# A four-layer graph network on one core: list building in layer 0 at one and a half steps per group instead of two

## The chip, the cores and the metric

The kernel runs on one core of a Trainium2 chip. The metric is the device time of one launch in microseconds (us): 1701.81 us, the median of three runs (1696.1 to 1703.36).

## The reference, cut to what matters

A graph of 3327 nodes has an adjacency matrix `adj` of ones and zeros and node features `x` of width 512. Four layers follow each other; each computes `x = layernorm(x + layer(x, adj))`.

```python
# layer 0: attention with 8 heads of 64
Wh = einsum('nd,hdo->hno', x, W);  f1 = Wh . a1;  f2 = Wh . a2
e = leaky_relu(f1[:, :, None] + f2[:, None, :], 0.2), where adj > 0, else -9e15
out = elu(softmax(e) @ Wh)
# layer 1: mean over all neighbours, two dense products, one combining product, relu
# layer 2: mean over the first 64 neighbours, a dense product on each side, leaky relu
# layer 3: attention with 4 heads of 128 on a quaternion weight
```

Edges are many in the first rows and few in the last: node i is joined to node j with a chance proportional to 1/sqrt((1+i)(1+j)).

## The kernel before, in words

**Tiling.** The nodes are cut into 26 blocks of 128. For blocks 1 to 25 the kernel doesn't use the dense matrix: it builds an edge list for each block (`lists`, a class `EdgeList`), with one entry per edge, in chunks of 128 edges. Block 0, the densest, is treated apart, with whole rows of the matrix (`dense`).

**List building** is the Python generator `structure` (its instructions are on lines 861 to 982). For each block it fetches the adjacency rows (L874, two halves on the SP queue, one pair of buffers), takes their sign on ScalarE (L881, `masks`), multiplies by a position code (L896), finds the columns with repeated maxima on VectorE (L909, L919, L921), counts places with small matmuls (L931, L932, L943), spreads them to edge places with matmuls `pv` (L960) and comparisons (L968 to L975), and writes the list (L978 to L981). It stops (`yield`) five times per block, so a list is five steps. The function `more(n)` takes n such steps; `ready` is the place, in the order of blocks, of the last list that is done.

**Layer 0** has two stages. In the first, 26 blocks are loaded, transposed and multiplied by the weights, and a table `t0_d` of rows is written; each block brings three steps of list building. In the second, the table's rows are gathered, edge by edge. A loop goes over groups of up to four chunks (`feed`, `groups`): there are 63 such groups, for 201 chunks in all, in 25 blocks. A group is a generator too (`Gat.group`): gathers on POOL (L1005), distances on ScalarE (L1267), choice of edges on VectorE (L1275, L1277), scores on TensorE (L1287) and transposed choice (L1297), reduction and maximum on VectorE (L1303 to L1306), exponentials on ScalarE (L1307, L1308), a copy of the choice to SBUF (L1310), the multiply of gathered rows by the weights on VectorE (L1315, one per group), and the sums on TensorE (L1334). When a block's groups are done its end follows (`layer0_end`): normalization on VectorE and ScalarE (L1485 to L1498, L857), and two dense products into `po` (L797) whose results go to `t1_d` and `z1_d` through the SP queue.

**The loop around the change** takes one group, moves every living generator one stage on (`work.step()`), and then calls `more`. At its start 17 of 26 places are ready, so nine lists, 45 steps, are left. A group whose list isn't ready yet would build on demand:

```python
            while ready < order.index(item[0]):
                more()
            work.add(g0.group(item, pools, accs, layer0))
        work.step()
        more(2)
```

When the last list is done (`ready == NB - 1`), the buffers of the building are closed, and their space goes to weights of layer 2, which are loaded (L1688) and transposed on TensorE (L1697) and copied by ScalarE (L1698) as one more generator, `transposed_weights`. Block 0's dense work (L1437, L1444) starts with the last seven blocks, when 18 of 25 blocks have been passed on.

**What sets the order.** The program text isn't the order on the engines. In layer 0 a scheduler at build time places each engine's instructions, by their dependences and the order in which they were written; every engine then runs its own list in order. From layer 1 on the order is that of the text. In the second stage of layer 0 the pool `l0p1` has one buffer for each of its names, and `banks.shared` gives the building's matmuls `pv` the buffer `po` of the dense products, and its transposes and sums (`lp`) the buffer `tr` of the transposes.

Of the kernel before, what the change touches and what calls it, by code (L numbers as in the profile page):

```python
# [631 lines left out]
def sparse_path(ctx, tc, flag_i, x, adj, l0_w, l0_a1, l0_a2, l1_w_self, l1_b_self, l1_w_nb, l1_b_nb,  # L632
# [26 lines left out]
    def pool_in(lay, name, bufs=1, **kw):  # L659
        return lay.enter_context(tc.tile_pool(name=name, bufs=bufs, reuse_waits="tile", **kw))  # L660
# [880 lines left out]
    with ExitStack() as pro:  # L1541
# [83 lines left out]
        def more(n=1):  # L1625
            nonlocal ready, whole
            for k in range(n):
                b = next(made, None)
                whole = b is not None or ready == NB - 1
                ready = ready if b is None else b  # L1630
# [50 lines left out]
    def transposed_weights():  # L1681

        n = len(raws) - 2
        jobs = [(src, o, k) for src, o in ((l2_w_nb, wn2), (l2_w_line, wl2)) for k in range(DC)]

        def fetch(i):
            src, _, k = jobs[i]
            nc.sync.dma_start(raws[i % n], src[k * P:(k + 1) * P, :])  # L1688

        for i in range(n):  # L1690
            fetch(i)
        yield
        for i, (_, o, k) in enumerate(jobs):
            yield
            pt = ps.tile([P, DC, P], F32, name="pt", tag="tr")
            for c in range(DC):
                nc.tensor.transpose(pt[:, c, :], raws[i % n][:, c * P:(c + 1) * P], ident)  # L1697
            nc.scalar.copy(o[:, :, k * P:(k + 1) * P], pt)  # L1698
            if i + n < len(jobs):
                fetch(i + n)  # L1700

    w2lay, dlay = ExitStack(), ExitStack()
    def feed():

        left = list(range(NB))
        blocks = [b for b in order if b]
        for n, b in enumerate(blocks):
            if n == len(blocks) - DENSE - 2:
                assert wn2 is not None
                dp = pool_in(dlay, "l0d")  # L1710
                work.add(g0.open_dense(fin, ps, pools[2], dp.tile([P, H0 * P], F32, name="up"),
                                       *[raws[-1 - k] for k in range(2)],
                                       *[dp.tile([P, H0 * g0.M], F32, name=f"gd{k}") for k in range(3)]))
            for item in groups(pools[0], (b,), True):
                yield item
                for _ in range(2):
                    if left and n >= len(blocks) - DENSE:
                        yield left.pop(0)
        yield from left

    for k, item in enumerate(feed()):
        if isinstance(item, int):
            work.add(g0.dense(item, fin, ps, pools[2], layer0))
        else:
            while ready < order.index(item[0]):
                more()
            work.add(g0.group(item, pools, accs, layer0))
        work.step()
        more(2)
        if ready == NB - 1 and wn2 is None:  # L1730
            listlay.close()
            aside = pool_in(ctx, "s_more")
            wp = pool_in(w2lay, "l2w")
            wn2 = wp.tile([P, DC, D], F32, name="wn2")
            wl2 = wp.tile([P, DC, D], F32, name="wl2")
            places = aside.tile([P, MORE], F32, name="raw", tag="aside")
            raws = [places[:, k * D:(k + 1) * D] for k in range(2)]
            raws += [places[:, (k + 1) * H0 * P:(k + 2) * H0 * P] for k in range(2)]
            work.add(transposed_weights())
# [356 lines left out]
@with_exitstack  # L2096
def kernel(ctx: ExitStack, tc: tile.TileContext, *args):


    nc = tc.nc  # L2100
    pool = ctx.enter_context(tc.tile_pool(name="flagp", bufs=1))
    flag_i = pool.tile([1, 1], I32, name="flag_i")
    sparse_path(tc, flag_i, *args)
    again = nc.values_load(flag_i[0:1, 0:1], min_val=0, max_val=1 << 20)
    with tc.If(again > 0):
        general_path(tc, *args)
# [30 lines left out]
```

## Time and profile before

| what | value |
|---|---|
| median of three runs | 1701.81 us |
| the profiled execution, its time | 1795.35 us |
| its span, first to last instruction | 1793.6 us |
| TensorE busy | 1513.9 us, 84% |
| VectorE busy | 1220.8 us, 68% |
| ScalarE busy | 876.6 us, 49% |
| POOL busy | 762.9 us, 43% |
| mean granted TensorE clock | 0.932 |
| groups of gathers of layer 0 (L1315) | 250 to 713 us |
| last write of an edge list (L980) | 398 us |

How to read it: times in the profile count from the first instruction of the span. A line such as L1315 is a line of the kernel's text; PE is TensorE's matmul, PEld its weight load, DVE is VectorE, ACT is ScalarE, POOL is GpSimd, SP is the engine that only issues transfers. A row of a group gives engine, operation, output and inputs with their shapes, how often it ran, its busy time and mean duration, and the engine's idle time just before it with what ended most of it. Row sums of VectorE and ScalarE are larger than the engine's busy time, because one instruction's end overlaps the next one's start. The busy time of TensorE is modelled, and a busy TensorE isn't one at its peak.

### The profile page before, as it was taken

Reading aid. Unit: us, or ns where it says so; the run is one execution under the profiler, and the core shown is the slowest. Engines: PE = TensorE matmul, PEld = TensorE weight load, DVE = VectorE, ACT = ScalarE, POOL = GpSimd, SP = SyncE. Lnnn points to the kernel's source line nnn. Section 1 sums busy time; section 2 is a strip of 40 time slices with the busy share of each in tenths; the row PEclk is TensorE's granted clock in tenths of the full one; section 3 lists DMA queues with packets and bytes.
Section 4 is the critical chain, followed back from the end, with each engine's and each line's share of the span. In section 5 each row is a group of like instructions: output and inputs, shape, how many; then the busy total and the mean of one; then the engine's idle time right before and its main releaser. Section 6 shows DMA issues by size and latency. Waiting matters only on the chain. (4 is left out here: it accounts for less than half of the span.)

```text
span 1793.6 us, 24341 instructions
## 1 busy us (share of the span) xinstructions
PE 1513.9 (84%) x7263; PEld 1007.8 (56%) x7298; DVE 1220.8 (68%) x3289; ACT 876.6 (49%) x2921; POOL 762.9 (43%) x904
## 2 busy tenths in 40 slices
PE   5979937789999999889999998856999984788784
PEld 4756526556666667345555554423666662666663
DVE  8989859996668788135665675537655533687896
ACT  5879645656566677311221221102444442476785
POOL 2000144555555510264545552366667106666540
PEclk9989968999999999989999998988999995999897
DMA  8787766766564531398889894387888207677761
GB/s 265 248 266 241 210 192 232 207 189 205 173 200 153 178 113 61 144 401 289 291 283 357 274 319 182 132 285 246 260 263 278 92 37 199 196 209 211 214 182 44
DMA packets 130402, 381.99 MB, mean 213 GB/s; under 512 B 22037, under 2 KB 36477, under 8 KB 130259
## 3 DMA queue, kind: packets, MB, share of 16 engines
q0 software_dynamic: 67696, 252.97, 44.8%
q1 hardware_dynamic: 62563, 127.35, 21.1%
q8 instruction: 60, 0.98, 0.2%
q14 instruction: 83, 0.68, 0.1%
HBM read 331.89 MB, written 48.37 MB: 212 GB/s over the span
## 5 line engine op out<-in xcount | busy, mean ns | idle before, releaser
L1005 POOL DMA_INDIRECT gl<-t_d,idx x270 | 270.5, 1002 | 272.2 <-DMA e_d<-es 81.0
L1005 POOL DMA_INDIRECT gt<-t_d,idx x201 | 200.5, 998 | 377.4 <-DVE g0fall L845 199.7
L1334 PE MATMUL acc<-gt,sel 128*128 128x264 f32 (+3 forms) x804 | 213.0, 412 | 3.1 <-issue 1.8
L797 PE MATMUL po<-wn,xt 128*128 128x512 f32 x416 | 193.6, 607 | 11.0 <-ACT xt L785 5.7
L1005 POOL DMA_INDIRECT gm<-t_d,idx x136 | 137.7, 1012 | 136.9 <-PE acc L1810 81.8
L1334 PEld LDWEIGHTS acc<-gt,sel 128*128 128x128 f32 (+3 forms) x804 | 154.4, 201 | 43.9 <-issue 17.0
L1334 PE MATMUL acc<-gl,sel 128*128 128x260 f32 (+3 forms) x544 | 147.6, 416 | 29.5 <-issue 21.9
L1334 PEld LDWEIGHTS acc<-gl,sel 128*128 128x128 f32 (+3 forms) x544 | 105.9, 204 | 52.4 <-issue 26.1
L797 PEld LDWEIGHTS po<-wn,xt 128*128 128x128 f32 x416 | 78.7, 195 | 94.6 <-issue 76.2
L1042 PE MATMUL po<-gt,xt 128*128 128x268 f32 x416 | 115.7, 423 | 14.8 <-ACT xt L789 11.2
L1315 DVE TENSOR_TENSOR gt<-gt,pg 128x1536 f32<-128x1536 f32 (+3 forms) x63 | 116.4, 1848 | 15.4 <-ACT sel L1310 14.7
L785 ACT COPY xt<-pt 128x512 f32<-128x512 f32 x81 | 46.7, 588 | 140.3 <-PE pt L782 108.4
L1810 PE MATMUL acc<-gm,selr 128*128 128x512 f32 (+4 forms) x324 | 107.2, 454 | 5.4 <-DMA gm<-t_d,idx 3.6
L909 DVE MAX8 cand<-val 128x8 f32<-128x464 uint16 (+32 forms) x184 | 107.7, 619 | 0.0
L1042 PE MATMUL po<-w,xt 128*128 128x262 f32 x416 | 99.5, 393 | 6.3 <-ACT xt L789 5.1
L1042 PEld LDWEIGHTS po<-gt,xt 128*128 128x128 f32 x416 | 78.4, 202 | 34.1 <-ACT xt L789 14.5
L1267 ACT ACTIVATE far<-place,nmids 128x128 int16<-128x128 int16 (+3 forms) x167 | 88.0, 544 | 18.2 <-DVE ds L1277 10.1
L797 PE MATMUL po<-wx,xt 128*128 128x512 f32 x208 | 93.7, 595 | 2.1 <-DVE t L1669 1.8
L797 PE MATMUL po<-wl,xt 128*128 128x512 f32 x208 | 93.5, 594 | 2.0 <-DVE tb L1877 1.3
L1042 PEld LDWEIGHTS po<-w,xt 128*128 128x128 f32 x416 | 78.8, 192 | 25.2 <-ACT xt L789 7.5
L782 PE MATMUL pt<-s_ident,xres 128*128 128x128 f32 x500 | 79.1, 287 | 13.3 <-DVE xres L852 10.0
L881 ACT ACTIVATE m<-ab 128x1664 bf16<-128x1664 int32 x50 | 80.2, 1605 | 16.9 <-DMA ab<-in_adj_dram 13.2
(372 smaller groups left out, 3238.8 us busy)
## 6 DMA issues: line engine op xcount, KB each, us to landing
ab<-in_adj_dram SPq DMA_DIRECT2D x25, 832.0 KB
ab<-in_adj_dram SPq DMA_DIRECT2D x25, 831.5 KB
t_d<-t SPq DMA_DIRECT2D x25, 512.0 KB
gm<-t_d POOLq DMA_DIRECT2D x25, 512.0 KB
t_d<-t SPq DMA_DIRECT2D x25, 384.0 KB
t_d<-tg SPq DMA_DIRECT2D x25, 264.0 KB
gd<-t_d SPq DMA_DIRECT2D x25, 264.0 KB
t_d<-tg SPq DMA_DIRECT2D x25, 260.0 KB
```

The lines of the kernel that those rows point to most:

```text
L782: nc.tensor.transpose(pt[:, c, :], src[:, c * P:(c + 1) * P], ident)
L785: nc.scalar.copy(xt, pt)
L797: nc.tensor.matmul(po, xt[:, c, :], w[:, c], start=c == 0, stop=c == DC - 1)
L881: nc.scalar.activation(m, ab[s], AF.Sign, accum_out=half[:, s, b:b + 1])
L909: nc.vector.max(out=cand[:, s, :], in_=val[:, cuts[s]:cuts[s + 1]])
L1005: nc.gpsimd.indirect_dma_start(out=t[:m, c, :], out_offset=None, in_=table[:, :], in_offset=bass.IndirectOffsetOnAxis(ap=l.idx[:m, c0 + c: ...
L1042: nc.tensor.matmul(pw[s], xt[:, c, :], self.w[:, c, s, :], start=c == 0, stop=c == DC - 1)
L1267: nc.scalar.activation(o, place[:, (c0 + q0) * P:(c0 + q1) * P], AF.Abs, bias=l.nmid[:, k:k + 1], scale=2.0)
L1315: nc.vector.tensor_mul(Gc[:, :, :OUT], Gc[:, :, :OUT], w[:, :g].rearrange("p c (h o) -> p (c h) o", o=1).to_broadcast([P, g * H, OUT]))
L1334: nc.tensor.matmul(accs[b][s], S[:m, c, :], G[:m, c, s * hh * M:(s + 1) * hh * M], start=at + c == 0, stop=last)
L1810: nc.tensor.matmul(accs[b], chosen, parts[:, k * D:(k + 1) * D], start=at + c + k == 0, stop=k == top and at + c == n - 1)
```

## The change

The loop takes one step of list building after every even group and two after every odd one. The 45 steps then end with the 30th group instead of the 23rd; the eight transposes of layer 2's weights, which follow the last list, begin that many groups later. The dense work of block 0 keeps its place.

```diff
             work.add(g0.group(item, pools, accs, layer0))
         work.step()
-        more(2)
+        more(1 + k % 2)
         if ready == NB - 1 and wn2 is None:
             listlay.close()
             aside = pool_in(ctx, "s_more")
```

## The prediction

> **What bounds the kernel now.** I first read the busy shares of the page in forty slices of 44.8 us, to find the stage that the edit touches. Groups of gathers run from about 250 us to 713 us; list building among them ends at about 398 us, where the last write of an edge list (L980) stands. That is slices 5 to 8 (counted from 0).
>
> ```profile
> PE   5979937789999999889999998856999984788784
> DVE  8989859996668788135665675537655533687896
> PEclk9989968999999999989999998988999995999897
> ```
>
> Slices 6 to 8 have VectorE at 9 and TensorE at 7 or 8; from slice 9 TensorE is at 9 and VectorE falls to 6. So I cut the trace at 405, 455 and 545 us, and asked for the busy times (columns: length, PE, PEld, DVE, ACT, POOL, clock, DMA share, GB/s).
>
> ```profile
> 250.00:405.00 155.00, 122.75 (x656) 89.72 (x657) 140.40 (x471) 93.70 (x276) 77.53 (x82) 0.88 0.68 206
> 405.00:455.00 50.00, 50.00 (x240) 34.55 (x240) 32.35 (x80) 33.52 (x105) 26.38 (x30) 1.00 0.68 205
> 455.00:545.00 90.00, 89.18 (x380) 58.54 (x379) 60.38 (x150) 54.59 (x169) 51.17 (x64) 1.00 0.59 182
> ```
>
> While lists are built VectorE is busy 140.4 of 155 us (90.6%) and TensorE 122.75; afterwards TensorE has no idle time at all. Then the waits of TensorE in 250 to 405 us (total us, times, longest):
>
> ```profile
> PE pg L1287 <- DVE gt L1315: 23.6, 9, 8.8
> PE p L931 <- DVE dg L929: 4.3, 2, 3.3
> PE pv L960 <- ACT u L953: 2.5, 1, 2.5
> PE pv L960 <- ACT dl L945: 2.4, 2, 2.1
> PE po L797 <- DVE t L1669: 1.5, 1, 1.5
> PE pv L960 <- ACT vc L963: 1.4, 1, 1.4
> PE po L797 <- ACT vc L963: 1.2, 2, 0.9
> ```
>
> TensorE waits chiefly for VectorE's multiply of gathered rows (L1315), the one big VectorE instruction of each group. In 405 to 455 us the same view has no wait of TensorE. Last, VectorE's costliest groups in 250 to 405 us, and the transposes of layer 2's weights, which follow the building:
>
> ```profile
> L1315 DVE TENSOR_TENSOR gt<-gt,pg 128x2048 f32<-128x2048 f32 (+1 forms) x22 | 44.3, 2012 | 0.3 <-ACT sel L1310 0.3
> L909 DVE MAX8 cand<-val 128x8 f32<-128x1018 uint16 (+5 forms) x43 | 30.4, 736 | 0.0
> L896 DVE TENSOR_TENSOR val<-m,code 128x1664 uint16<-128x1664 bf16 x14 | 14.1, 1011 | 0.0
> L946 DVE TENSOR_TENSOR dl<-p,dl 128x26 bf16<-128x26 f32 x9 | 1.6, 182 | 4.5 <-ACT dl L945 3.7 <-issue 0.7
> ...
> L1697 PE MATMUL pt<-s_ident,raw x32: 272/273/421, 397.2 to 448.5; 128*128 128x128 f32 x32
> ```
>
> Two stages, then: 23 groups in 160 us (the first L1315 starts at 250, the 23rd at 410), 7.0 us each, set by VectorE; and from there 22 groups in 135 us (the 45th at 545), 6.1 us each, set by TensorE.
>
> **What the Trainium skill says.** "Perfetto Trace Analysis", Optimization Strategy: a kernel may have regimes with different most-contended engines, and interleaving them may help. The trace has just these two regimes. "TensorE: Matmul & The Clock Gate", Part 1: an idle window of about 3.4 us puts the clock back to half. The trace agrees in direction: with waits up to 8.8 us the granted clock was 0.88 in the first stage, and 1.00 afterwards. The same page's table has VectorE as a strict first-in first-out queue; the L946 row agrees (4.5 us idle in nine places with other groups' work behind). "Perfetto Trace Analysis", Matmuls: independent matmul groups should rotate through PSUM banks. Here the building's pv and the dense products' po share one buffer, and the waits of po for vc (1.2 us) and for t (1.5 us) are that price so far.
>
> **The change part by part.** Nothing is computed anew: the same 45 steps (nine lists of five) stay, one or two per group in turn instead of two. They are used up in 30 groups instead of 23. Sizes and waits on `ready` stay the same: in program order no group comes to the loop that builds on demand, in either kernel (list 17 is due before block 17, which begins with the 46th group). What moves is read from the order of instructions on each engine, which is the same again from about the 39th group on.
>
> VectorE. Ahead of the 23rd L1315 stand 946 building instructions in the kernel before, 899 in the changed one: 47 fewer, among them two L896, six L909, 39 small ones. By the rows: 2 x 1.01 + 6 x 0.74 + 39 x 0.19 (the small rows run 0.15 to 0.25) = 13.9 us. Row sums overlap: all VectorE rows of 250 to 405 us add up to 176 us where the engine is busy 140.4, so times 0.80, 11 us. At 90.6% use that brings the 23rd group from 410 to 398 us: **-12 us**. But by the 25th L1315 only 23 small ones are missing (23 x 0.19 x 0.8 = 3.5 us): the order lets two L896 and six L909 catch up between groups 23 and 25. Between these VectorE has then 11 - 3.5 = 7.5 us of building on top of 2.5 us for each group (the group's rows add up to 70.5 us for 23, times 0.80) and one layer end of 3.2 us (15.8 us for four, times 0.80): 16 us, where the kernel before took 10 us (410 to 420). So the 25th group comes at 414 instead of 420: **-6 us**.
>
> TensorE. From there it sets the pace in both. By the 25th group the kernel before had done 20 of the 32 weight transposes, the changed one none. All 32 took 5.3 us busy (1.06 up to 405 us, 4.23 after), so 20 cost 3.3 us, and the last 12 of the pv matmuls 0.7 us (7.0 us for 120 in their row): **+4 us**, uncovered, because TensorE has no idle time left to hide them. Before, some of the transposes went into its idle time before 405 us.
>
> Waits. TensorE's waits on the building (p, pv, and po behind vc) were 4.3 + 2.5 + 2.4 + 1.4 + 1.2 = 11.8 us for eight lists, 1.5 us a list, then free behind VectorE. About 0.7 of a list's small tail falls into TensorE's stage: **+1 us**; bounds 0 and, if each is lengthened threefold by a fuller ScalarE queue, 3.
>
> Clock. The first groups meet TensorE less idle, so its clock may rise sooner; VectorE sets the pace there, so I take 0, with 2 us of gain as the bound.
>
> DMA. Of SP, the last two lists' adjacency loads (L874) now stand after stores of t1 and z1, and the weight loads (L1688) among later stores. The store ahead of such a load waits for a result whose ScalarE part stands ahead of the mask that frees the load's own buffer, so the queue adds nothing I can find: 0. Without that cover a late load holds mask L881 at the head of ScalarE, and everything behind it; one load lasts about 10 us, for at most two lists. POOL's gathers keep their order; two memsets (L872) and square roots move among them by a few places: 0.
>
> Sum: -6 + 4 + 1 = **-1 us** of the profiled execution. Two favourable roundings stand beside it: VectorE may run the long catch-up above 95% busy (-1), and some transposes may slip into TensorE's waits on the last lists (-1). I take -3. That execution took 1795.35 us, with a span of 1793.6; the median of the runs is 1701.81, 5.2% less. A shift of 3 us carries over as 3 us: **1699 us**. Dense work of row 0 and everything after the 39th group has the same order, and starts 3 us sooner.
>
> **The rivals.**
>
> *The relief is kept.* VectorE's work is evened out and TensorE follows. 250 to 455 us have 140.4 + 32.35 = 172.75 us of VectorE; at 90.6% that is 190.7 us instead of 205, -14; transposes +5, so -9. If chains of small building steps also hide better between groups (VectorE at 95%: 182 us), -18. Middle: 1688 us. For it: 32 us of TensorE idle in the first stage. Against: the order gives back most of the building by the 25th group.
>
> *The first stage keeps its pace, and the second pays.* If the first 23 groups are held by latencies from engine to engine, not by VectorE's work, taking half a step from each saves nothing. Then all 32 transposes and the waits and pv matmuls of 2.2 lists (at the 20th L1315, 70 building instructions of some 31 a list are missing) land where TensorE is full: 5.3 + 2.2 x 1.5 + 1 = +10, so 1712 us. It decides from the point where the first 25 groups gain less than the 4 to 5 us that TensorE is handed. For it: of the fourteen ten-us windows from 250 to 390 us, four show VectorE at 87% or less. Against: 90.6% over all.
>
> *Nothing is seen.* List building has slack everywhere: 1702 us. It falls in with my forecast within the measurement.
>
> **How the numbers follow.** My forecast, with the case of no effect, has 0.5 (own range 1693 to 1709), the kept relief 0.24, the payment 0.26. One half per cent (8.5 us: 1693.3 to 1710.3) is about what a measurement of this kernel can tell from no change. The relief case lies mostly below, the payment case mostly above, a little of each inside, and a little of the forecast outside: faster 0.23, same 0.52, slower 0.25. The range reaches to the middle of each rival and somewhat beyond on the slow side, for a late load: 1685 to 1717.
>
> **What would show it.** Right: the 23rd L1315 starts some 12 us earlier than 410, the 25th some 6, the 35th 2 or 3; VectorE is above 85% busy until about 430 us, transposes (L1697) run from about 445 to 490 us, TensorE has new waits there for vc, u or dl; from the 45th group all intervals are as before. Wrong on the good side: TensorE's total wait in 250 to 455 us drops by over 10 us. Wrong on the bad side: the 25th group is not earlier, or masks (L881) wait for the adjacency. If dense work (L1444) changes its intervals, I have missed a dependence altogether.

## The result, and the profile after

| | before | changed |
|---|---|---|
| median of 13 runs | 1701.69 us | 1692.47 us |
| lowest to highest | 1695.88 to 1704.8 us | 1687.15 to 1695.45 us |
| ratio to before, 95% interval | 1 | 0.9947, 0.9934 to 0.9959 |
| the profiled execution, its time | 1795.35 us | 1689.52 us |

The changed kernel is 9.2 us (0.53%) faster. The two first profiles can't be subtracted: that of before comes from an execution of 1795 us, that of the changed kernel from one of 1690 us. In the later experiments the runs of both kernels took some 1790 us, and there the ratio came out the same (0.995). So the stages are compared on profiles from those, one of each kernel.

First the page of the changed kernel's first profile, busy shares in forty slices (of 42.2 us, since its span is 1687.8 us):

```profile
PE   5979987989999989889999999787999996888884
DVE  7998979988668789316556677547666644789996
PEclk9989989999999999879999999899999997999998
```

From slice 6 on VectorE has 9, 9, 8, 8, 6, and TensorE 7, 9, 8, 9, 9; before it was 9, 9, 9, 6, 6 and 7, 7, 8, 9, 9. The step from one engine to the other is softer. (The slices of the two pages differ in length, so this is no more than an impression.)

Now the pair: a further profile of the kernel before (span 1783.2 us) and one of the changed kernel (1788.8 us). The pair understates the gain. The execution of before was 5.5 us shorter than the median of the runs taken with it (1790.46), that of the changed kernel 3.1 us longer than its own (1787.47). Both profiles are cut at the start of the first, 23rd, 30th and 45th L1315, rounded to whole microseconds (columns: length, PE, PEld, DVE, ACT, POOL, clock, DMA share, GB/s). The kernel before:

```profile
249.00:408.00 159.00, 126.99 (x678) 92.19 (x679) 142.09 (x480) 98.29 (x293) 80.74 (x84) 0.89 0.68 209
408.00:452.00 44.00, 44.00 (x217) 31.25 (x216) 29.44 (x68) 27.41 (x82) 23.57 (x27) 1.00 0.66 198
452.00:542.00 90.00, 89.59 (x382) 58.86 (x381) 61.03 (x150) 55.16 (x173) 52.07 (x64) 1.00 0.60 184
```

The changed kernel:

```profile
248.00:393.00 145.00, 119.93 (x640) 86.86 (x641) 130.03 (x412) 89.25 (x256) 81.04 (x84) 0.92 0.70 219
393.00:441.00 48.00, 44.52 (x222) 30.56 (x222) 39.68 (x130) 31.22 (x108) 24.92 (x28) 0.96 0.66 195
441.00:537.00 96.00, 94.05 (x415) 62.14 (x413) 64.02 (x156) 60.19 (x184) 51.22 (x62) 1.00 0.61 185
```

The stretch to the 23rd group is 14 us shorter (13.2 before rounding), with 12 us less of VectorE's work in them. The next seven carry 10 us more of it and take 4 us longer, and the fifteen after that take 6 us longer: the weight transposes stand there now. In the stretch as a whole TensorE is idle for 30.5 us instead of 32.4 (length less busy, the three rows added), and its busy time is 258.5 us instead of 260.6, with a higher granted clock in the first row (0.92 for 0.89) and a lower one in the second (0.96 for 1.00).

The waits of TensorE, before, in the first row's window (total us, times, longest):

```profile
PE pg L1287 <- DVE gt L1315: 14.9, 8, 4.2
PE pg L1287 <- DVE nmids L940: 6.7, 1, 6.7
PE p L931 <- DVE dg L929: 3.3, 1, 3.3
```

And the two largest of the changed kernel in its first row, 248 to 393 us:

```profile
PE pg L1287 <- DVE gt L1315: 14.2, 7, 5.6
PE po L797 <- issue: 4.0, 1, 4.0
```

TensorE's idle time in the first row falls from 32.0 to 25.1 us, but the wait that the prediction named first, for L1315, is as long as before. What has gone is chiefly the one wait of 6.7 us behind the building's `nmids`. The changed kernel's waits in its second and third rows, 393 to 537 us:

```profile
PE pg L1287 <- DVE gt L1315: 1.7, 2, 0.8
PE pt L1697 <- ACT xt L785: 1.1, 1, 1.1
PE pt L782 <- ACT xres L857: 0.9, 1, 0.9
PE pt L782 <- ACT wn L1698: 0.7, 1, 0.7
PE pv L960 <- ACT u L953: 0.5, 1, 0.5
```

These are small waits where TensorE was full before: one on the building (u), two on VectorE's multiply, the others on ScalarE's work for the layer ends and the transposes. None is long.

### The profile page after: what moved, and what is told of

Read it like the earlier page. It is cut to its first block, busy times and chain, and to the rows that moved or that the text cites. A ratio compares the mean times of both kernels' runs of the same rounds, so it can differ in the third digit from the quotient of the medians.

```text
span 1687.8 us, 24368 instructions
## 1 busy us (share of the span) xinstructions
PE 1490.9 (88%) x7298; PEld 994.6 (59%) x7298; DVE 1220.4 (72%) x3289; ACT 874.4 (52%) x2921; POOL 767.4 (45%) x904
## 5 line engine op out<-in xcount | busy, mean ns | idle before, releaser
L1005 POOL DMA_INDIRECT gl<-t_d,idx x270 | 274.2, 1015 | 221.9 <-DMA e_d<-es 80.6
L1334 PE MATMUL acc<-gt,sel 128*128 128x264 f32 (+3 forms) x804 | 208.7, 405 | 3.7 <-issue 1.8
L797 PE MATMUL po<-wn,xt 128*128 128x512 f32 x416 | 195.5, 613 | 11.6 <-ACT vc L963 4.9
L1334 PEld LDWEIGHTS acc<-gt,sel 128*128 128x128 f32 (+3 forms) x804 | 151.0, 197 | 39.6 <-issue 13.4
L1334 PE MATMUL acc<-gl,sel 128*128 128x260 f32 (+3 forms) x544 | 140.8, 405 | 27.1 <-issue 14.9
L797 PEld LDWEIGHTS po<-wn,xt 128*128 128x128 f32 x416 | 79.4, 196 | 96.7 <-issue 77.5
L1334 PEld LDWEIGHTS acc<-gl,sel 128*128 128x128 f32 (+3 forms) x544 | 102.6, 198 | 44.5 <-issue 15.6
L1315 DVE TENSOR_TENSOR gt<-gt,pg 128x1536 f32<-128x1536 f32 (+3 forms) x63 | 116.3, 1847 | 13.6 <-ACT sel L1310 13.4
L1042 PE MATMUL po<-gt,xt 128*128 128x268 f32 x416 | 111.4, 410 | 15.5 <-ACT xt L789 11.6
L797 PE MATMUL po<-wl,xt 128*128 128x512 f32 x208 | 93.4, 594 | 0.7 <-ACT xt L785 0.7
L797 PE MATMUL po<-wx,xt 128*128 128x512 f32 x208 | 93.5, 594 | 0.0
L881 ACT ACTIVATE m<-ab 128x1664 bf16<-128x1664 int32 x50 | 80.1, 1603 | 16.8 <-DMA ab<-in_adj_dram 12.5
```

What stands on the lines that cost most here:

```text
L797: nc.tensor.matmul(po, xt[:, c, :], w[:, c], start=c == 0, stop=c == DC - 1)
L881: nc.scalar.activation(m, ab[s], AF.Sign, accum_out=half[:, s, b:b + 1])
L1005: nc.gpsimd.indirect_dma_start(out=t[:m, c, :], out_offset=None, in_=table[:, :], in_offset=bass.IndirectOffsetOnAxis(ap=l.idx[:m, c0 + c: ...
L1042: nc.tensor.matmul(pw[s], xt[:, c, :], self.w[:, c, s, :], start=c == 0, stop=c == DC - 1)
L1315: nc.vector.tensor_mul(Gc[:, :, :OUT], Gc[:, :, :OUT], w[:, :g].rearrange("p c (h o) -> p (c h) o", o=1).to_broadcast([P, g * H, OUT]))
L1334: nc.tensor.matmul(accs[b][s], S[:m, c, :], G[:m, c, s * hh * M:(s + 1) * hh * M], start=at + c == 0, stop=last)
```

## The experiments

Two theories stood against each other from the start. **The spread:** VectorE's work sets the pace while lists are built, so building fewer steps per group shortens that stage, and TensorE's full stage takes the rest in. **The transposes:** what helps is that they move. A third, **an accident of the order**, says that any new order from the scheduler shifts the time by a few microseconds.

**The kernel before again, twice** (no edit), for profiles under the conditions of the other runs.

> The kernel before, once more, for a second profile: the first one's execution took 1795 us where the runs take 1702. If that execution was disturbed from outside, this one has a span near 1702 us, and its first 23 groups take some 148 us, not 160; if profiling itself slows this kernel, it has 1790 us again.

> The kernel before, for the profile that stands against the changed kernel's on this chip: 1700 or 1785 us, by the chip; 23rd group 145 to 160 us after the first.

Measured: 1784.97 and 1803.47 us, spans 1783.2 and 1801.7. So some 1790 us is the kernel's own time in these experiments, not an odd profile. The 23rd group starts 158.8 and 166.9 us after the first (159.6 in the first profile), the 45th 293.0 and 304.6 us (294.5). In the longer one VectorE stands idle for longer in the first stage. Its longest waits between 249 and 416 us (second of the two runs):

```profile
DVE off L968 <- ACT vc L963: 6.0, 4, 1.9
DVE off L968 <- issue: 5.3, 2, 3.8
```

VectorE stands still in the building's own chain, at the step that needs the result of a matmul that ScalarE copies (vc). In the shorter execution the same stage has 17 us of idle VectorE in all, here 25. What the first stage takes in the kernel before thus varies by several microseconds from one execution to the next.

**The changed kernel again**, beside the second of these.

> The changed kernel, beside a kernel before on the same chip, for a pair of profiles. Theory of the spread: the 23rd group some 12 to 15 us earlier counted from the first, the 25th 6 to 9, the 45th 3 to 6, and the time 5 to 9 us less. If the first result's 9 us was more than the spread gives, the 45th group is 10 us or more earlier; where does that come in?

Measured: ratio 0.995 (0.9934 to 0.9966), 9 us of 1797.81. Counted from the first L1315, the 23rd starts at 145.6 us, the 25th at 162.7, the 30th at 193.5, the 35th at 230.3, the 45th at 289.2. Against the shorter profile of before (158.8, 169.4, 202.8, 234.8, 293.0) that is -13.2, -6.7, -9.3, -4.5 and -3.8 us; against the mean of the three (161.8, 172.4, 205.9, 239.1, 297.4) it is -16, -10, -12, -9 and -8 us. The runs' 9 us agree with the mean better than with the shorter profile.

**The transposes late, the building as before.**

```diff
-        if ready == NB - 1 and wn2 is None:
+        if ready == NB - 1 and wn2 is None and k >= 29:
```

> Two steps per group as before, but the transposes of layer 2's weights begin with the 30th group, as in the changed kernel. Theory of the spread (the gain comes from VectorE being relieved in the first stage): not faster than before, 0 to +4 us, the price of the later transposes. Theory of the transposes (the gain comes from their moving away from the first layer ends): most of the 9 us gain, 1693 to 1695 us.

Measured: ratio 0.9991 (0.9973 to 1.0008), so -1.6 us, between -4.8 and +1.4. The theory of the transposes falls: moved alone, to where the changed kernel has them, they give at most half of the gain and on the median almost nothing. They don't show a cost either. Their line in this kernel:

```profile
L1697 PE MATMUL pt<-s_ident,raw x32: 271/273/328, 448.5 to 492.4; 128*128 128x128 f32 x32
```

They really ran some 45 to 50 us later (before: 397 to 448 us). The same stretches, again between the first, 23rd, 30th and 45th L1315:

```profile
251.00:409.00 158.00, 123.40 (x674) 88.73 (x675) 142.51 (x482) 98.81 (x297) 79.59 (x84) 0.92 0.68 210
409.00:450.00 41.00, 41.00 (x192) 28.84 (x191) 29.23 (x68) 23.43 (x72) 23.09 (x27) 1.00 0.60 181
450.00:545.00 95.00, 93.34 (x411) 61.80 (x410) 61.43 (x151) 59.31 (x182) 52.34 (x65) 1.00 0.62 191
```

Of the 5 us that the third row is longer than in the kernel before (95 against 90), 4 come off the two rows ahead of it (41 against 44, 158 against 159): TensorE was full in the second row already, so the transposes had a price in their old place too.

**VectorE's price in each stage.** In the kernel before, VectorE repeats its choice of edges, with the same operands and result, four times instead of once, in the first 22 groups (pad1: 81 repeats, of 365 columns on the mean) or in groups 24 to 45 (pad2: 90, of 299 columns). The rest of the edit, which fills the set `pads`, is cut here.

```diff
                 elif q0 < q1:
-                    nc.vector.tensor_scalar(o, t[:, q0 * P:q1 * P], dk, None, ALU.is_lt)
+                    for _ in range(4 if (b, at) in self.pads else 1):
+                        nc.vector.tensor_scalar(o, t[:, q0 * P:q1 * P], dk, None, ALU.is_lt)
```

> The kernel before with 81 idle repeats of VectorE's choice of edges (L1277, some 0.3 us each) in the first 22 groups: 24 us of row sums, 19 us of VectorE. Theory of the spread (VectorE's work sets the first stage): +15 to +21 us. Rival, the first stage is held by latencies from engine to engine: under +8 us.

> The same with 90 repeats (some 0.27 us each, 19 us of VectorE) in groups 24 to 45, where TensorE is full. Theory of the spread (VectorE work is free there): 0 to +4 us. Rival, VectorE's latency counts there as well: +10 us or more, and then moving list building there would not pay.

Measured: pad1 1.0094 (1.0061 to 1.0127; three runs), +17 us of 1797.81, pad2 1.0034 (1.0013 to 1.0054), +6 us. The +17 is clear of the rival that latencies hold the first stage (under 8); the +6 is more than the 0 to 4 expected and less than the 10 of its rival. The row of pad1 between its first and 23rd L1315, and that of pad2 between its 23rd and 45th:

```profile
250.00:421.00 171.00, 127.38 (x657) 91.14 (x654) 156.18 (x544) 95.02 (x276) 80.00 (x83) 0.86 0.63 188
```

```profile
409.00:549.00 140.00, 135.36 (x603) 90.71 (x602) 106.41 (x293) 84.75 (x256) 76.35 (x89) 1.00 0.62 182
```

In the first stage 14 us more of VectorE (156.18 against 142.09) lengthen it by 12 us in the trace, and the runs by 17: it is paid about one for one. (By the 25th group the trace has 16 us, 185.2 after the first against 169.4; TensorE has more of its own work between the two groups there.) In the second, 16 us more (106.41 against 90.47 in 134 us before) lengthen it by 6 us: cheap, not free. TensorE has 4.6 us of idle time there in place of 0.4. So the spread is right about where VectorE's work counts. An estimate from these traces: 12 us of VectorE less in the first stage, at pad1's rate of 12/14, is -10 us, and as much more in the second, at 6/16, is +5, together -5; with the runs' 17/14 in the first stage it is -15 and +5, together -10. Idle repeats stand for VectorE's share alone: the building that moves also brings matmuls and ScalarE's work along.

**The phase of the pattern**, with the same mean rate.

```diff
-        more(2)
+        more(2 - k % 2)
```

> One and a half steps per group, but two after even groups and one after odd ones. Theory of the spread: the same gain as the changed kernel, 1690 to 1695 us. Theory of an accident of the order (any new order moves the time by some us either way): a time that differs from the changed kernel's by 5 us or more.

Measured: ratio 0.9978 (0.9965 to 0.9991), -4 us. Its stages are those of the changed kernel (23rd group 144.3 us after the first, 45th 287.6), but its runs show half the gain. Whether that is the order isn't shown. The two phases were not run side by side (medians 1785.68 beside 1790.46 of before, 1787.47 beside 1797.81), their intervals touch, and the kernel with one step per group, run twice further down, gave 0.9909 and 0.9936: one and the same program came out as far apart as the two phases.

**Other rates.** The notes behind # are mine.

```diff
-        more(2)
+        more(3)                     # r3: 15 groups
+        more(1 + (k % 3 == 2))      # r43: 34 groups
+        more(1 + (k % 4 == 3))      # r54: 36 groups
+        more(1)                     # r1, r1b: 45 groups
```

> Three steps per group, so the 45 steps end with the 15th group. Theory of the spread: VectorE holds the first stage more strictly, TensorE waits more: +8 to +15 us. Theory of an accident of the order: anything within 5 us of before.

> One step, and two after every third group: 34 groups. Theory of the spread: a little more gain than one and a half steps, -9 to -14 us. Theory of the accident: no order among the rates.

> One step, and two after every fourth group: 36 groups; the transposes then end just before block 0's dense work. Theory of the spread: between the rates of four thirds and one, -10 to -16 us. If dense work in the way of the transposes costs something at one step per group, this one is the fastest.

> One step per group: the 45 steps end with the 45th group. Theory of the spread: at least as fast as one and a half steps as far as VectorE goes, -9 to -15 us, unless the transposes then fall together with block 0's dense work; with the late transposes as the price: +4 us more than at one and a half, so about -5 us. Theory of the accident: no order among the rates.

> One step per group again, beside the other rates on one chip; the first time it was 15 us faster with six runs. Theory of the spread: again -12 to -18 us.

Each ratio is to the runs of before taken with it; their medians were 1790.46, 1797.81 and 1795.45 us.

| steps per group | ratio to before | 95% interval | 23rd and 45th group, us after the first |
|---|---|---|---|
| 3 | 1.0077 | 1.0046 to 1.0107 | 175.5, 309.5 |
| 2 (before, three profiles) | 1 | | 158.8 to 166.9, 293.0 to 304.6 |
| 1.5 (the change) | 0.9950 | 0.9934 to 0.9966 | 145.6, 289.2 |
| 1.5, other phase | 0.9978 | 0.9965 to 0.9991 | 144.3, 287.6 |
| 4/3 | 0.9911 | 0.9879 to 0.9943 | 137.0, 284.2 |
| 5/4 | 0.9979 | 0.9959 to 0.9999 | 134.8, 286.4 |
| 1, first time | 0.9909 | 0.9879 to 0.9939 | 133.9, 278.8 |
| 1, second time | 0.9936 | 0.9914 to 0.9957 | 134.9, 281.7 |

The first stage gets shorter with every step down to 5/4, and what is left at the 45th group follows with one exception, 5/4. The theory of the accident, no order among the rates, falls. Three steps came as expected (+14 us), four thirds gained 16 us where 9 to 14 were expected, one step 16 and 11 us where 9 to 15 and 12 to 18 were. One step beats the kernel before; its ratios are also below that of the changed kernel (0.9909 and 0.9936 against 0.9950), but the two were not run side by side.

The rate of 5/4 missed its expectation of 10 to 16 us by far (4 us), and beside 4/3 and 1 in the same runs it is the one real exception. In its profile most of the difference to 4/3 lies outside the stage that the edit touches: 2 us at the 45th group, 3 at the last of the 63, and 9 more behind it (1085.8 against 1076.8 us), where VectorE, ScalarE and POOL have their instructions in the same order in all these kernels. In the three profiles of before this last stretch took 1074.0 to 1081.1 us. Why 5/4 loses there in its 21 runs too, if it is there, stays open.

The ends of the scale, between first and 23rd L1315: three steps, as a whole and cut at the 15th L1315, ahead of which its last list is written (L980, 363.8 us), and then one step (second run):

```profile
252.00:427.00 175.00, 132.74 (x692) 97.98 (x691) 142.58 (x472) 104.28 (x304) 78.34 (x83) 0.84 0.63 194
252.00:377.00 125.00, 85.74 (x466) 63.63 (x465) 114.19 (x409) 74.93 (x213) 51.45 (x53) 0.79 0.62 192
377.00:427.00 50.00, 47.00 (x228) 34.35 (x227) 28.39 (x64) 29.35 (x93) 26.89 (x30) 0.97 0.65 199
```

```profile
247.00:382.00 135.00, 117.04 (x601) 85.87 (x602) 111.54 (x326) 78.77 (x232) 75.04 (x82) 0.91 0.71 215
```

With three steps TensorE is idle for 42 us and gets a clock of 0.84; with one, for 18 us, at 0.91. VectorE's busy time is the same at three steps as at two, 142 us, because all the building was inside the stage already, and yet the stage is 16 us longer than in the shorter profile of before. The cut shows why: up to the 15th group VectorE is busy for 114 of 125 us and TensorE waits; behind it TensorE is busy for 47 of 50 us and VectorE is idle for 22. The earlier the building ends, the more groups run with VectorE's time unused.

## Why the prediction was right, point by point

**Direction and bound.** 1699 us was forecast, with 1685 to 1717; 1692.47 came. The gain was three times the 3 us forecast: the median lies just below my own range (1693 to 1709), just past the half per cent that I had set for "faster", and nearer to the 1688 us of the kept relief than to my 1699. The wide range, drawn to the middles of the rivals, took it in. The direction, VectorE's relief ahead of the 23rd group, was argued and came; the size was not. The theory it rests on, two stages with VectorE and TensorE in turn, is shown by the two padded kernels.

**VectorE: -12 us at the 23rd group, -6 at the 25th.** -13.2 and -6.7 in the pair; the count of instructions, 11 us less, shows as 12 us less of busy VectorE. Against the mean of three profiles it is -16 and -10. The term was sized on one execution, and the kernel before varies there; by the means this is about half of the gain that the sum missed. Two small readings were off: from the first to the 23rd L1315 there are 22 intervals, so 7.3 us a group and not 7.0, and the 4.5 us of idle VectorE at L946 came before three of its nine runs.

**TensorE: +4 us for the transposes, "uncovered".** This is the step that failed. The transposes run where I said (440 to 485 us, forecast 445 to 490). But by the start of the 25th L1315 the kernel before has done 12 of the 32 and not 20, and TensorE didn't have to stand by while VectorE caught up. From the 25th to the 45th L1315, before (the shorter profile) and then changed:

```profile
418.30:541.90 123.60, 123.19 (x549) 82.56 (x547) 82.53 (x197) 74.60 (x224) 69.37 (x82) 1.00 0.62 187
410.60:537.10 126.50, 123.25 (x557) 82.27 (x556) 87.94 (x243) 81.94 (x260) 65.70 (x79) 0.99 0.63 190
```

TensorE has the same busy time, 123.2 us, though all 32 transposes are in the second row and 20 in the first. Between the 23rd and the 25th group it worked for 14.9 us, 10.6 us before, and did sums (L1334) and dense products (L797) ahead of time: 12 and 5 fewer of them are left for the second row. So nothing uncovered is seen there, and the late transposes alone moved the time by -1.6 us, +1.4 at most.

**Waits: +1, up to 3 us.** The second row is 2.9 us longer, and all of it is idle TensorE (3.3 us, before 0.4), so the term came at its bound; between the 23rd and the 25th group there are 2.2 us more. In the lines shown for 393 to 537 us only 0.5 of 4.9 us is a wait on the building itself (u). I had counted only such waits. The building also delays other work on VectorE and ScalarE for which TensorE waits; pad2, without any building moved, has 4.6 us of idle TensorE.

So the sum was right in the pair by errors that cancel: -6.7 and +2.9 make -3.8 at the 45th group, where I had -6, +4, +1 and two roundings of -1, together -3. Against the mean of three profiles of before the same parts are -9.7 and +1.5, together -8, near the runs' 9: there both steps, -6 and +5, were mis-sized.

**Clock: 0, with 2 us of gain as the bound.** The clock of the first stage went from 0.89 to 0.92, and TensorE's busy time up to the 45th group fell by 2.1 us for as many recorded matmuls (1277). That is the bound itself, and in the sum of busy and idle time it stands as one half of the pair's 4 us; the fall in idle time, 1.9 us, is the other. That the clock alone shortened the busy time isn't shown.

**SP's queue: 0.** In the changed kernel no load holds ScalarE: from 260 us on the masks (L881) have idle time before them only for VectorE's L896, 1.5 us. One wait on a transfer does reach TensorE: at 379.2 us ScalarE's L1495 has stood 2.4 us for the store `z_d<-zb`, with the copy vc behind it, and TensorE's dense product starts at 379.9 us after 4.0 us of idle time. The kernel before has such waits of L1495 too (2.6 us in 405 to 455 us), so it isn't shown that the change made it.

**The rivals.** "The first stage keeps its pace" fell: it became 13 us shorter. "The relief is kept" came nearer than I gave it credit for: -9 was its lower end, by its own sum of VectorE's 172.75 us. Its middle, 1688 us, was too much.

**What stays open.** The runs show 9 us. The pair has 4 us at the 45th group and 1.4 us at the last of the 63 (458.9 against 460.3 after the first); against the mean of three profiles of before it is 8 and 7 us. A single profile has no better resolution here: two spans of before under the same conditions were 1783.2 and 1801.7 us. How much of the 9 us belongs to the rate and how much to this one order isn't settled; the other phase, with 4 us (2 to 6), leaves room for about half.

## What to carry to other kernels

When a background task runs beside the main loop, look at each stretch for the engine that is full, and try rates at which the task ends later, up to just before it is needed: here each step down from three to 5/4 shortened the stretch where VectorE was full, and idle repeats on VectorE later, where TensorE was full, cost about four tenths of their length (6 us for 16). Price moved work in its old place before counting it as a debt: 32 transposes that moved from one place where TensorE was full to another showed no cost in the runs. Look also at what an engine can bring forward while it would wait. And run variants side by side before ranking them: two sets of runs of one program differed by 0.3% here (0.9909 and 0.9936), and one rate out of five fell out of line by some 0.5% without a known cause.

## What the runs showed of the hardware that was not expected

The same two kernels took about 1700 and 1692 us in the first comparison and some 1790 us in all later ones, which used two chips; what makes the difference isn't known. In the changed kernel's profile of 1687.8 us there is one stretch of over 1 us in which TensorE (matmuls and weight loads), VectorE and ScalarE all stand still (6.1 us, at the start); in its profile of 1788.8 us there are 13, 44 us together, while its span is 101 us longer. The longest, of 9.5 us, comes when POOL starts on layer 0's first gathers. From the timeline of that profile (start, duration, instruction, idle time before it):

```profile
230.43 0.95 POOL L1005 DMA_INDIRECT gt<-t_d,idx  x1 [0.30 <-issue]
...
235.55 0.27 ACT L963 CAST vc<-pv 128x135 int16<-128x135 f32 x1 [10.91 <-remote]
...
236.28 0.29 PE L960 MATMUL pv<-dl,u 128*128 128x27 bf16 x4 [10.94 <-issue]
```

POOL issues a gather every 1.25 us throughout; the three others have nothing that they are seen to wait for. Between 200 and 250 us that profile has 25.57 us of busy TensorE, the faster one 40.24. What stops the engines was not tried. Both kernels have it (14 to 18 such stretches, 42 to 48 us together, in the three profiles of before), and the ratio is the same with and without it (0.9947 and 0.9950).
